# A graph layer's edge gather: three of sixteen columns moved from indirect DMAs to one-hot matmuls

## The chip, the cores and the metric

The kernel runs on one core of one Trainium2 chip. The metric is the device time of one execution in microseconds. Before the change it is 2046.08 us, the median of 3 runs (2045.63 to 2046.55).

The core has five engines that run side by side, each in the order of its own instruction stream: TensorE (PE in the profile, its weight loads PEld), VectorE (DVE), ScalarE (ACT), GpSimd (POOL) and SyncE (SP). They wait for each other by semaphores. On-chip memory is SBUF, with 128 partitions; matmuls write to PSUM[...].

## The reference

```python
# x: 6250 x 64; src, dst: 206250 edges, sorted by dst; edge_attr: 206250 x 64
h = maximum(layernorm(x), 0)
msg = relu(h[src] + edge_attr)
agg = segment_sum(msg, dst, num_segments=6250)
out = x + relu((h + agg) @ W1 + b1) @ W2 + b2
```

All is fp32. The edges are sorted by destination, so edges that lie next to each other add into nodes that lie next to each other. The source indices are random.

## The kernel before

**Groups and columns.** Edges are taken in 201 groups of 1024 (`GE`): partition p holds 8 consecutive edges (`G`), so a group is 8 columns of 128 edges. A last group of 4 columns holds the tail. The source and destination indices of all columns are loaded at the start (`src_sb`, `dst_sb`).

**Prologue.** `ln_head`, `ln_rows` and `ln_turn` compute h in chunks of 12 x 128 nodes. Each chunk is written to DRAM (`h_rows`) and is also turned by TensorE into `z`, which holds h with features on partitions and nodes along the row; the sums are added into `z`. The first 4 groups (`RAW`) gather rows of x, not of h, and are normalized after the gather (`norm_edges`), so that they need not wait for h.

**Loading.** `load(g)` issues one 256 KB load of attributes on SP's queue and, in `gather` (L133), one indirect DMA on GpSimd's queue for each column: 128 rows of 64 floats, chosen by that column's indices. The buffers `ea` and `xg` are 12 deep (`LOOK`), so gathers run ahead of the compute until no buffer is free.

**A group's compute.** `take(g+1)` lets ScalarE copy the next group's attributes into PSUM (`full`, L306). `window_sum(g)` then does the following. VectorE builds the one-hot of each edge's place in a window of 64 nodes (`oh`, L318), adds the gathered rows to `full` (L322), and ScalarE takes the relu. The message is split into three bf16 terms that add up to the fp32 value (L324 to L328, alternating between ScalarE and VectorE). TensorE sums the 8 columns by matmuls with the one-hot as the stationary operand (L333), giving a tile of 64 nodes x 3 x 64. `turn(g)` runs two groups later (`TLAG`): VectorE adds the three terms (L288) and TensorE transposes the result (L292). `sum_into_z(g)` runs six groups later (`LAG`): VectorE adds the 64 columns into `z` at a start that it reads from `dst_sb` into a register (L297); the registers are loaded for 8 groups at a time.

**Blocks.** When all edges of a block of 512 nodes have surely been summed (`READY`), `hidden` (L341, L343), `result` (L351) and `store` (L358) compute and write its output, in steps two groups apart (`blocks_behind`).

**Order.** The schedule is written by hand: each engine executes its instructions in the order in which the loop at the end of the kernel issues them. No planner moves them.

**Left-over edges.** `find_left` and `judge` look for edges that do not fit their group's window, and a slow path behind a condition handles those. With these inputs it is not entered.

Of the kernel before, what the change touches and what calls it, by code (L numbers as in the profile page):

```python
# [9 lines left out]
F32 = mybir.dt.float32  # L10
I32 = mybir.dt.int32
BF16 = mybir.dt.bfloat16
# [24 lines left out]
LOOK = 12  # L37
LAG = 6
TLAG = 2
AB = 2  # L40
TB = 4
# [7 lines left out]
def kernel(  # L49
# [18 lines left out]
    lnp = ctx.enter_context(tc.tile_pool(name="ln", bufs=2))  # L68
    edge = ctx.enter_context(tc.tile_pool(name="edge", bufs=LOOK))
    work = ctx.enter_context(tc.tile_pool(name="work", bufs=4))  # L70
# [45 lines left out]


# [18 lines left out]

    def load(g):
        ea = edge.tile([P, G, D], F32, name="ea")
        attr_load(ea, g)
        xg = edge.tile([P, G, D], F32, name="xg")  # L140
        gather(xg, src_sb[:, cols_of(g)], G if g < NG else CT, x if g < RAW else h_rows)
        return ea, xg
# [5 lines left out]

    def norm_edges(xg):
        s = lnp.tile([P, XC * R], F32, name="ln_s")  # L150
        nc.vector.tensor_reduce(s[:, :G], xg, AX.X, ALU.add)
        nc.vector.tensor_scalar_mul(s[:, :G], s[:, :G], 1.0 / D)
        nc.vector.tensor_tensor(xg, xg, s[:, :G].unsqueeze(2).to_broadcast([P, G, D]), ALU.subtract)
        sq = lnp.tile([P, XC * R, D], F32, name="ln_sq")
        nc.scalar.activation(sq[:, :G], xg, AF.Square)
        v = lnp.tile([P, XC * R], F32, name="ln_v")
        nc.vector.tensor_reduce(v[:, :G], sq[:, :G], AX.X, ALU.add)
        nc.scalar.activation(v[:, :G], v[:, :G], AF.Sqrt, bias=eps_sb, scale=1.0 / D)
        nc.vector.reciprocal(v[:, :G], v[:, :G])
        nc.vector.scalar_tensor_tensor(xg, xg, 0.0, v[:, :G].unsqueeze(2).to_broadcast([P, G, D]),  # L160
                                       op0=ALU.max, op1=ALU.mult)
# [13 lines left out]
    def ln_rows(c, xc, sq, p, n):  # L175
        v = lnp.tile([P, XC * R], F32, name="ln_v")
        nc.vector.tensor_reduce(v[:p, :n], sq[:p, :n], AX.X, ALU.add)
        nc.scalar.activation(v[:p, :n], v[:p, :n], AF.Sqrt, bias=eps_sb[:p], scale=1.0 / D)
        nc.vector.reciprocal(v[:p, :n], v[:p, :n])
        h = lnp.tile([P, XC * R, D], F32, name="ln_h", bufs=3)  # L180
        nc.vector.scalar_tensor_tensor(h[:p, :n], xc[:p, :n], 0.0,  # L181
                                       v[:p, :n].unsqueeze(2).to_broadcast([p, n, D]),
                                       op0=ALU.max, op1=ALU.mult)
        if c < NB:
            nc.sync.dma_start(
                out=h_rows[c * P * R:(c + XC) * P * R, :].rearrange("(b p r) d -> p b (r d)", p=P, r=R),
                in_=h.rearrange("p (b r) d -> p b (r d)", r=R),
            )
        else:
            nc.sync.dma_start(out=h_rows[NB * P * R:, :], in_=h[:TN, 0, :])  # L190
        return c, h

# [13 lines left out]
    for c in range(0, NB + 1, XC):  # L206
        heads.append(ln_head(c))
        if len(heads) > 1:
            rows.append(ln_rows(*heads[-2]))
        if len(rows) > 1:  # L210
            ln_turn(*rows[-2])
    rows.append(ln_rows(*heads[-1]))
    ln_turn(*rows[-2])
    ln_turn(*rows[-1])
# [26 lines left out]
    found = {}  # L241

    def find_left():
        nc.vector.tensor_scalar(left, slot, 1.0, None, op0=ALU.is_lt)
        nc.vector.scalar_tensor_tensor(left, slot, float(W), left, op0=ALU.is_gt, op1=ALU.add)
        nc.vector.scalar_tensor_tensor(left, dst_sb, 1.0, left, op0=ALU.add, op1=ALU.mult)
        nc.vector.memset(left[:TD, C + TJ:], 0.0)
        most = const.tile([P, 1], F32, name="most")
        nc.vector.tensor_reduce(most, left, AX.X, ALU.max)
        pf = psum.tile([P, R * D], F32, name="big", bufs=1)  # L250
        nc.tensor.matmul(pf[0:1, 0:1], most, ones[:, 0:1], start=True, stop=True)
        found["all"] = pf

    def judge():
        pf = found.pop("all")
# [23 lines left out]
    aggs = {}  # L279

    turned = {}
    banks = []
    turns = []

    def turn(g):
        pa = aggs.pop(g)
        rows = work.tile([W, D], F32, name="agg_rows", bufs=LAG)
        nc.vector.tensor_reduce(rows, pa.rearrange("w t d -> w d t"), AX.X, ALU.add)  # L288
        if g % TB == 0:
            turns.append(psum.tile([D, TB, W], F32, name="turned", bufs=2))  # L290
        pt = turns[-1][:, g % TB]
        nc.tensor.transpose(pt, rows, ident[:W, :W])  # L292
        turned[g] = pt

    def sum_into_z(g):
        at = window_start(g)
        nc.vector.tensor_tensor(z[:, ds(at, W)], z[:, ds(at, W)], turned.pop(g), ALU.add)  # L297

    taken = {}

    def take(g):

        n = G if g < NG else CT
# [3 lines left out]
        taken[g] = full, xg  # L307

    def window_sum(g):
        n = G if g < NG else CT  # L310
        cols = cols_of(g)
        if g + 1 <= NG:
            take(g + 1)
        full, xg = taken.pop(g)
        if g < RAW:
            norm_edges(xg)
        oh = work.tile([P, G, W], BF16, name="oh")
        nc.vector.tensor_tensor(  # L318
            oh[:, :n], slot[:, cols].unsqueeze(2).to_broadcast([P, n, W]),
            wslots.unsqueeze(1).to_broadcast([P, n, W]), ALU.is_equal)  # L320

        nc.vector.tensor_tensor(full[:, :n], full[:, :n], xg[:, :n], ALU.add)  # L322
# [5 lines left out]
        nc.vector.tensor_tensor(parts[:, :n, 2, :], full[:, :n], parts[:, :n, 1, :], ALU.subtract)  # L328
        if g % AB == 0:
            banks.append(psum.tile([W, AB, 3, D], F32, name="agg", bufs=2))  # L330
        pa = banks[-1][:, g % AB]
        for j in range(n):
            nc.tensor.matmul(pa, oh[:, j, :], parts[:, j], start=(j == 0), stop=(j == n - 1))  # L333
# [41 lines left out]

    take(0)
    for g in range(NG + 1):
        window_sum(g)
        if g >= TLAG:
            turn(g - TLAG)  # L380
        if g >= LAG:
            sum_into_z(g - LAG)
            blocks_behind(g - LAG)
        if g == 8:
            find_left()
        if g == 14:
            judge()
        if g == 15:
# [4 lines left out]
    for g in range(NG + 1 - TLAG, NG + 1):  # L393
        turn(g)
# [4 lines left out]
    for c in sorted(res):  # L399
        store(c, res.pop(c))  # L400
# [76 lines left out]
```

## Time and profile before

| | |
|---|---|
| median of 3 runs | 2046.08 us |
| profiled execution | 2045.61 us |
| its span, first to last instruction | 2043.8 us |
| instructions in it | 10215 |
| busy: TensorE, its weight loads | 402.8 us, 294.9 us |
| busy: VectorE, ScalarE, GpSimd | 669.9 us, 386.5 us, 1530.5 us |
| indirect gathers (L133) | 1580 from h_rows, 32 from x |
| moved by DMA | 112.98 MB, 55 GB/s over the span |

The profile is that of one execution. A row of its table of groups gives the line, the engine, the operation, the tiles written and read, the shapes and the count; then the busy time in us and the mean duration of one instruction in ns; then the time that the engine sat idle just before these instructions, and what ended most of that idle time. "issue" means that nothing the profile shows was waited for. Lines of the timeline give the start in us, the duration in us, the engine and the group, and in brackets the idle time before it.

### The profile page before, as it was taken

Reading aid. Unit: us, or ns where it says so; the run is one execution under the profiler, and the core shown is the slowest. Engines: PE = TensorE matmul, PEld = TensorE weight load, DVE = VectorE, ACT = ScalarE, POOL = GpSimd, SP = SyncE. Lnnn points to the kernel's source line nnn. Section 1 sums busy time; section 2 is a strip of 40 time slices with the busy share of each in tenths; the row PEclk is TensorE's granted clock in tenths of the full one; section 3 lists DMA queues with packets and bytes.
Section 4 is the critical chain, followed back from the end, with each engine's and each line's share of the span. In section 5 each row is a group of like instructions: output and inputs, shape, how many; then the busy total and the mean of one; then the engine's idle time right before and its main releaser. Section 6 shows DMA issues by size and latency. Waiting matters only on the chain. (4 is left out here: it accounts for less than half of the span.)

```text
span 2043.8 us, 10215 instructions
## 1 busy us (share of the span) xinstructions
PE 402.8 (20%) x1991; PEld 294.9 (14%) x1991; DVE 669.9 (33%) x1321; ACT 386.5 (19%) x652; POOL 1530.5 (75%) x1619
## 2 busy tenths in 40 slices
PE   2221121121121121112112112212111211211212
PEld 1111111111111111111111111111111111111111
DVE  4643333333333333332333333333333233333333
ACT  3321111111111111111111111111111111111111
POOL 7777777777777777777777777777777777777774
DMA  5221113113113113111311411311311221131121
GB/s 184 69 56 41 26 27 111 27 26 116 27 27 106 32 27 101 42 27 26 111 27 26 117 27 27 106 32 27 106 37 27 66 72 26 28 115 26 27 62 23
DMA packets 87529, 112.98 MB, mean 55 GB/s; under 512 B 30948, under 2 KB 35684, under 8 KB 87460
## 3 DMA queue, kind: packets, MB, share of 16 engines
q0 software_dynamic: 51584, 52.93, 13.3%
q1 hardware_dynamic: 34628, 57.65, 8.5%
q10 hardware_dynamic: 1248, 1.70, 0.2%
q14 instruction: 52, 0.43, 0.1%
q8 instruction: 17, 0.28, 0.1%
HBM read 108.96 MB, written 3.20 MB: 55 GB/s over the span
## 5 line engine op out<-in xcount | busy, mean ns | idle before, releaser
L133 POOL DMA_INDIRECT xg<-h_rows,src_sb x1580 | 1497.7, 948 | 481.5 <-issue 434.0
L333 PE MATMUL agg<-parts,oh 128*64 128x192 bf16 x1612 | 294.5, 363 | 1593.4 <-DVE parts L328 1593.4
L333 PEld LDWEIGHTS <-oh 128*64 128x64 bf16 x1612 | 237.7, 165 | 1634.9 <-DVE parts L328 783.6
L322 DVE TENSOR_TENSOR full<-full,xg 128x512 f32<-128x512 f32 x202 | 140.9, 698 | 957.8 <-DMA xg<-h_rows,src_sb 957.8
L324 ACT ACTIVATE parts<-full 128x512 bf16<-128x512 f32 x202 | 120.4, 596 | 1201.1 <-DVE full L322 1198.3
L325 DVE SCALAR_TENSOR_TENSOR full<-full,parts 128x512 f32<-128x512 f32 x202 | 141.1, 698 | 151.0 <-ACT parts L324 151.0
L328 DVE TENSOR_TENSOR parts<-full,parts 128x512 bf16<-128x512 f32 x202 | 139.5, 690 | 131.5 <-ACT parts L327 131.5
L306 ACT COPY full<-ea 128x512 f32<-128x512 f32 x202 | 118.6, 587 | 199.4 <-DVE parts L328 134.8
L327 ACT CAST parts<-full 128x512 bf16<-128x512 f32 x202 | 118.2, 585 | 154.6 <-DVE full L325 154.6
L318 DVE TENSOR_TENSOR oh<-slot,wslots 128x512 bf16<-128x512 f32 x202 | 135.4, 670 | 0.0
L297 DVE TENSOR_TENSOR z<-z,turned 64x64 f32 x202 | 41.2, 204 | 88.5 <-issue 86.3
L288 DVE TENSOR_REDUCE agg_rows<-agg 64x64 f32<-64x192 f32 x202 | 68.4, 339 | 0.5 <-PE agg L333 0.5
L292 PE MATMUL turned<-ident,agg_rows 64*64 64x64 f32 x202 | 63.0, 312 | 0.2 <-DVE agg_rows L288 0.2
L133 POOL DMA_INDIRECT xg<-in_x_dram,src_sb x32 | 31.7, 990 | 13.3 <-issue 9.4
L292 PEld LDWEIGHTS turned<-ident,agg_rows 64*64 64x64 f32 x202 | 25.4, 126 | 56.0 <-issue 52.4
L341 PE MATMUL big<-z,w_sb 64*64 64x512 f32 (+1 forms) x26 | 24.2, 1032 | 1.1 <-DVE z L297 0.6
L351 PE MATMUL big<-w_sb,h 64*128 64x64 f32 (+1 forms) x98 | 23.6, 418 | 1.2 <-ACT h L343 1.2
L351 PEld LDWEIGHTS big<-w_sb,h 64*128 64x128 f32 (+1 forms) x98 | 22.3, 329 | 3.2 <-ACT h L343 3.2
L199 PE MATMUL big<-ident,ln_h 128*64 128x128 f32 x48 | 12.7, 420 | 33.7 <-DVE ln_h L181 19.2
L343 ACT ACTIVATE h<-big,b_sb 64x512 f32<-64x512 f32 (+1 forms) x13 | 8.5, 656 | 56.6 <-PE big L341 56.6
L200 ACT COPY z<-big 64x512 f32<-64x512 f32 x12 | 12.6, 1051 | 11.5 <-PE big L199 11.5
L199 PEld LDWEIGHTS big<-ident,ln_h 128*64 128x64 f32 x48 | 6.4, 159 | 39.5 <-issue 19.1
(53 smaller groups left out, 69.1 us busy)
## 6 DMA issues: line engine op xcount, KB each, us to landing
ea<-in_edge_attr_dram SPq DMA_DIRECT2D x201, 256.0 KB
xg<-h_rows,src_sb POOLq DMA_INDIRECT x1580, 2.4
x_sb<-in_x_dram SPq DMA_DIRECT2D x4, 384.0 KB
h_rows<-ln_h SPq DMA_DIRECT2D x4, 384.0 KB
out_dram<-o SPq DMA_DIRECT2D x12, 128.0 KB
dst_sb<-in_dst_main_dram ACTq DMA_DIRECT2D x1, 804.0 KB
src_sb<-in_src_main_dram ACTq DMA_DIRECT2D x1, 788.0 KB
xg<-in_x_dram,src_sb POOLq DMA_INDIRECT x32, 2.5
```

The lines of the kernel that those rows point to most:

```text
L133: nc.gpsimd.indirect_dma_start(out=xg[:, j, :], out_offset=None, in_=rows[:, :], in_offset=bass.IndirectOffsetOnAxis(ap=idx[:, j:j + 1], a ...
L288: nc.vector.tensor_reduce(rows, pa.rearrange("w t d -> w d t"), AX.X, ALU.add)
L292: nc.tensor.transpose(pt, rows, ident[:W, :W])
L306: nc.scalar.copy(full[:, :n], ea[:, :n])
L318: nc.vector.tensor_tensor(oh[:, :n], slot[:, cols].unsqueeze(2).to_broadcast([P, n, W]), wslots.unsqueeze(1).to_broadcast([P, n, W]), ALU. ...
L322: nc.vector.tensor_tensor(full[:, :n], full[:, :n], xg[:, :n], ALU.add)
L324: nc.scalar.activation(parts[:, :n, 0, :], full[:, :n], AF.Relu)
L325: nc.vector.scalar_tensor_tensor(full[:, :n], full[:, :n], 0.0, parts[:, :n, 0, :], op0=ALU.max, op1=ALU.subtract)
L327: nc.scalar.copy(parts[:, :n, 1, :], full[:, :n])
L328: nc.vector.tensor_tensor(parts[:, :n, 2, :], full[:, :n], parts[:, :n, 1, :], ALU.subtract)
L333: nc.tensor.matmul(pa, oh[:, j, :], parts[:, j], start=(j == 0), stop=(j == n - 1))
L351: nc.tensor.matmul(p2[:p, k * D:(k + 1) * D], h1[:, k, :p], w2_sb, start=True, stop=True)
```

## The change

TensorE fetches some of the columns in place of GpSimd's indirect DMAs. From group 4 on, a group with an even number has its last 2 columns picked on chip and one with an odd number its last column: 3 of 16. The prologue keeps h in SBUF as three bf16 terms (`hp`, 49 sets of 128 nodes), and a table `ids` with the node number of each partition in each set. For a picked column, TensorE spreads its 128 source indices over all partitions (`spread`), VectorE compares them with `ids` in four instructions, which gives 49 one-hot matrices of 128 nodes x 128 edges, and TensorE multiplies each with its set of `hp`, adding up in one PSUM tile of 128 edges x 3 x 64 (`pick`). ScalarE puts the attributes into a fourth column of that tile, and VectorE's reduction over the four yields the sum of h and attribute for that column.

The window sum is rewritten with it: the messages stay fp32, and the message is now the stationary operand, so that the sum comes out with features on partitions. The split into bf16 terms, `turn` and its lag are gone. `sum_into_z` follows one group behind (`LAG` is 1), a block's stages follow one group apart, `judge` is part of `find_left`, `LOOK` is 10, and `one_hot(g + 1)` is built a group ahead.

```diff
-LOOK = 12
-LAG = 6
-TLAG = 2
-AB = 2
-TB = 4
+LOOK = 10
+LAG = 1
+AB = 4
+KB = NB * R + 1
+BIAS = 4096
+CUTS = (0, 13, 25, 37, KB)
...
+    node = const.tile([P, KB], I32, name="node")
+    nc.gpsimd.iota(node[:, :KB - 1].rearrange("p (b r) -> p b r", r=R), pattern=[[P * R, NB], [1, R]],
+                   base=BIAS, channel_multiplier=R)
+    nc.gpsimd.iota(node[:, KB - 1:], pattern=[[0, 1]], base=BIAS + NB * P * R, channel_multiplier=1)
+    ids = const.tile([P, KB, P], I16, name="ids")
+    hp = const.tile([P, KB, 3, D], BF16, name="hp")
+    nc.vector.memset(hp[:, KB - 1], 0.0)
...
+    def pool_cols(g):
+        if g == NG:
+            return CT
+        return G if g < RAW else G - 2 + g % 2
     def load(g):
         ea = edge.tile([P, G, D], F32, name="ea")
         attr_load(ea, g)
         xg = edge.tile([P, G, D], F32, name="xg")
-        gather(xg, src_sb[:, cols_of(g)], G if g < NG else CT, x if g < RAW else h_rows)
+        gather(xg, src_sb[:, cols_of(g)], pool_cols(g), x if g < RAW else h_rows)
         return ea, xg
...
+    def ln_parts(c, h):
+        p, k, n = (P, c * R, XC * R) if c < NB else (TN, KB - 1, 1)
+        nc.scalar.copy(hp[:p, k:k + n, 0, :], h[:p, :n])
+        rest = lnp.tile([P, XC * R, D], F32, name="ln_rest")
+        nc.vector.tensor_tensor(rest[:p, :n], h[:p, :n], hp[:p, k:k + n, 0, :], ALU.subtract)
+        nc.scalar.copy(hp[:p, k:k + n, 1, :], rest[:p, :n])
+        nc.vector.tensor_tensor(hp[:p, k:k + n, 2, :], rest[:p, :n], hp[:p, k:k + n, 1, :], ALU.subtract)
...
+        for c, h in rows:
+            ln_parts(c, h)
+    for k in range(0, KB, 7):
+        nc.scalar.copy(ids[:, k:k + 7], node[:, k:k + 7].unsqueeze(2).to_broadcast([P, 7, P]))
+    hot = ctx.enter_context(tc.tile_pool(name="hot", bufs=3))
...
-    aggs = {}
-    turned = {}
-    banks = []
-    turns = []
-    def turn(g):
-        pa = aggs.pop(g)
-        rows = work.tile([W, D], F32, name="agg_rows", bufs=LAG)
-        nc.vector.tensor_reduce(rows, pa.rearrange("w t d -> w d t"), AX.X, ALU.add)
-        if g % TB == 0:
-            turns.append(psum.tile([D, TB, W], F32, name="turned", bufs=2))
-        pt = turns[-1][:, g % TB]
-        nc.tensor.transpose(pt, rows, ident[:W, :W])
-        turned[g] = pt
+    tiles = [g * G + j for g in range(NG) for j in range(pool_cols(g), G)]
+    tile_no = {c: t for t, c in enumerate(tiles)}
+    ahead = {}
+    src16 = const.tile([P, C], I16, name="src16")
+    nc.vector.tensor_scalar_add(src16, src_sb[:, :C], float(BIAS))
+    turned = psum.tile([P, 8, P], BF16, name="turned", bufs=1)
+    def spread(t):
+        if t < len(tiles):
+            nc.tensor.transpose(turned[:, t % 8, :],
+                                src16[:, tiles[t]:tiles[t] + 1].bitcast(BF16).to_broadcast([P, P]), ident_b)
+    def pick(t):
+        oh = hot.tile([P, KB, P], BF16, name="hot")
+        at = turned[:, t % 8, :].bitcast(I16)
+        for k, to in zip(CUTS, CUTS[1:]):
+            nc.vector.tensor_tensor(oh[:, k:to], at.unsqueeze(1).to_broadcast([P, to - k, P]),
+                                    ids[:, k:to], ALU.is_equal)
+        pk = psum.tile([P, 4, D], F32, name="pick", bufs=2)
+        for k in range(KB):
+            nc.tensor.matmul(pk[:, :3], oh[:, k, :], hp[:, k], start=(k == 0), stop=(k == KB - 1))
+        return pk
...
+    aggs, hots, taken, picks, banks = {}, {}, {}, {}, []
     def sum_into_z(g):
         at = window_start(g)
-        nc.vector.tensor_tensor(z[:, ds(at, W)], z[:, ds(at, W)], turned.pop(g), ALU.add)
-    taken = {}
+        nc.vector.tensor_tensor(z[:, ds(at, W)], z[:, ds(at, W)], aggs.pop(g), ALU.add)
+    def one_hot(g):
+        n = G if g < NG else CT
+        oh = work.tile([P, G, W], F32, name="oh")
+        nc.vector.tensor_tensor(
+            oh[:, :n], slot[:, cols_of(g)].unsqueeze(2).to_broadcast([P, n, W]),
+            wslots.unsqueeze(1).to_broadcast([P, n, W]), ALU.is_equal)
+        hots[g] = oh
...
     def take(g):
-        n = G if g < NG else CT
+        n = pool_cols(g)
         ea, xg = loaded[g] if g < RAW else load(g)
         full = psum.tile([P, G, D], F32, name="full", bufs=2)
         nc.scalar.copy(full[:, :n], ea[:, :n])
-        taken[g] = full, xg
+        taken[g] = full, xg, ea
+    def pick_group(g):
+        for j in range(pool_cols(g), G if g < NG else 0):
+            t = tile_no[g * G + j]
+            spread(t + 4)
+            picks[g, j] = pick(t)
+            nc.scalar.copy(picks[g, j][:, 3], taken[g][2][:, j])
     def window_sum(g):
-        n = G if g < NG else CT
-        cols = cols_of(g)
-        if g + 1 <= NG:
-            take(g + 1)
-        full, xg = taken.pop(g)
+        n, m = (G, pool_cols(g)) if g < NG else (CT, CT)
+        full, xg, _ = taken.pop(g)
         if g < RAW:
             norm_edges(xg)
-        oh = work.tile([P, G, W], BF16, name="oh")
-        nc.vector.tensor_tensor(
-            oh[:, :n], slot[:, cols].unsqueeze(2).to_broadcast([P, n, W]),
-            wslots.unsqueeze(1).to_broadcast([P, n, W]), ALU.is_equal)
-        nc.vector.tensor_tensor(full[:, :n], full[:, :n], xg[:, :n], ALU.add)
-        parts = work.tile([P, G, 3, D], BF16, name="parts")
-        nc.scalar.activation(parts[:, :n, 0, :], full[:, :n], AF.Relu)
-        nc.vector.scalar_tensor_tensor(full[:, :n], full[:, :n], 0.0, parts[:, :n, 0, :],
-                                       op0=ALU.max, op1=ALU.subtract)
-        nc.scalar.copy(parts[:, :n, 1, :], full[:, :n])
-        nc.vector.tensor_tensor(parts[:, :n, 2, :], full[:, :n], parts[:, :n, 1, :], ALU.subtract)
+        nc.vector.tensor_tensor(full[:, :m], full[:, :m], xg[:, :m], ALU.add)
+        for j in range(m, n):
+            nc.vector.tensor_reduce(full[:, j], picks.pop((g, j)).rearrange("p t d -> p d t"), AX.X, ALU.add)
+        msg = work.tile([P, G, D], F32, name="msg")
+        nc.scalar.activation(msg[:, :n], full[:, :n], AF.Relu)
+        oh = hots.pop(g)
         if g % AB == 0:
-            banks.append(psum.tile([W, AB, 3, D], F32, name="agg", bufs=2))
+            banks.append(psum.tile([D, AB, W], F32, name="agg", bufs=1))
         pa = banks[-1][:, g % AB]
         for j in range(n):
-            nc.tensor.matmul(pa, oh[:, j, :], parts[:, j], start=(j == 0), stop=(j == n - 1))
+            nc.tensor.matmul(pa, msg[:, j, :], oh[:, j, :], start=(j == 0), stop=(j == n - 1))
         aggs[g] = pa
...
-    hid, res = {}, {}
+    hid = {}
     def blocks_behind(g):
-        for c in sorted(res):
-            if READY[c] + 4 <= g:
-                store(c, res.pop(c))
         for c in sorted(hid):
-            if READY[c] + 2 <= g and not res:
-                res[c] = result(c, hid.pop(c))
+            store(c, result(c, hid.pop(c)))
         for c in range(NB):
             if READY[c] == g:
                 hid[c] = hidden(c)
+    for t in range(4):
+        spread(t)
     take(0)
+    one_hot(0)
     for g in range(NG + 1):
-        window_sum(g)
-        if g >= TLAG:
-            turn(g - TLAG)
         if g >= LAG:
             sum_into_z(g - LAG)
             blocks_behind(g - LAG)
+        window_sum(g)
+        if g + 1 <= NG:
+            take(g + 1)
+            pick_group(g + 1)
+            one_hot(g + 1)
         if g == 8:
             find_left()
-        if g == 14:
-            judge()
-        if g == 15:
+        if g == 9:
             for c in range(NB):
                 nc.vector.tensor_tensor(x_sb[:, c], x_sb[:, c],
                                         b2_sb.unsqueeze(1).to_broadcast([P, R, D]), ALU.add)
             nc.vector.tensor_tensor(x_sb[:TN, NB, 0, :], x_sb[:TN, NB, 0, :], b2_sb[:TN], ALU.add)
-    for g in range(NG + 1 - TLAG, NG + 1):
-        turn(g)
     for g in range(NG + 1 - LAG, NG + 1):
         sum_into_z(g)
         blocks_behind(g)
```

More of the change, by code (lines that the diff above doesn't have):

```diff
@@ L11 @@
 I32 = mybir.dt.int32
+I16 = mybir.dt.int16
 BF16 = mybir.dt.bfloat16
@@ L67 @@
     const = ctx.enter_context(tc.tile_pool(name="const", bufs=1))
-    lnp = ctx.enter_context(tc.tile_pool(name="ln", bufs=2))
     edge = ctx.enter_context(tc.tile_pool(name="edge", bufs=LOOK))
-    work = ctx.enter_context(tc.tile_pool(name="work", bufs=4))
+    work = ctx.enter_context(tc.tile_pool(name="work", bufs=3))
     dram = ctx.enter_context(tc.tile_pool(name="dram", bufs=1, space=bass.MemoryType.DRAM))
@@ L115 @@
     nc.vector.tensor_copy(wslots, slots[:, :W])
+    ident_b = const.tile([P, P], BF16, name="ident_b")
+    nc.vector.tensor_copy(ident_b, ident)
+    node = const.tile([P, KB], I32, name="node")
[5 more added lines that the diff above has]
+    nc.vector.memset(hp[:, KB - 1], 0.0)
     h_rows = dram.tile([N, D], F32, name="h_rows")
@@ L147 @@
     loaded = [load(g) for g in range(RAW)]
[L149 to L161, printed above, removed]
     def ln_head(c):
@@ L179, in ln_rows @@
         nc.vector.reciprocal(v[:p, :n], v[:p, :n])
-        h = lnp.tile([P, XC * R, D], F32, name="ln_h", bufs=3)
+        h = lnp.tile([P, XC * R, D], F32, name="ln_h", bufs=5)
         nc.vector.scalar_tensor_tensor(h[:p, :n], xc[:p, :n], 0.0,
@@ L205 @@
     heads, rows = [], []
[L206 to L214, printed above, removed]
+    with tc.tile_pool(name="ln", bufs=2) as lnp:
+        for c in range(0, NB + 1, XC):
+            heads.append(ln_head(c))
+            if len(heads) > 1:
+                rows.append(ln_rows(*heads[-2]))
+            if len(rows) > 1:
+                ln_turn(*rows[-2])
+        rows.append(ln_rows(*heads[-1]))
+        ln_turn(*rows[-2])
+        ln_turn(*rows[-1])
+        for c, h in rows:
[3 more added lines that the diff above has]
+    hot = ctx.enter_context(tc.tile_pool(name="hot", bufs=3))
     base = const.tile([1, NG + 1], F32, name="base")
@@ L240 @@
     flag = const.tile([1, 1], I32, name="flag")
-    found = {}
     def find_left():
@@ L251, in find_left @@
         nc.tensor.matmul(pf[0:1, 0:1], most, ones[:, 0:1], start=True, stop=True)
-        found["all"] = pf
-    def judge():
-        pf = found.pop("all")
         done = const.tile([1, NG + 1], F32, name="done")
@@ new lines, in norm_edges @@
+    def norm_edges(xg):
+        s = hot.tile([P, G], F32, name="raw_s")
+        nc.vector.tensor_reduce(s, xg, AX.X, ALU.add)
+        nc.vector.tensor_scalar_mul(s, s, 1.0 / D)
+        nc.vector.tensor_tensor(xg, xg, s.unsqueeze(2).to_broadcast([P, G, D]), ALU.subtract)
+        sq = work.tile([P, G, D], F32, name="msg")
+        nc.scalar.activation(sq, xg, AF.Square)
+        v = hot.tile([P, G], F32, name="raw_v")
+        nc.vector.tensor_reduce(v, sq, AX.X, ALU.add)
+        nc.scalar.activation(v, v, AF.Sqrt, bias=eps_sb, scale=1.0 / D)
+        nc.vector.reciprocal(v, v)
+        nc.vector.scalar_tensor_tensor(xg, xg, 0.0, v.unsqueeze(2).to_broadcast([P, G, D]),
+                                       op0=ALU.max, op1=ALU.mult)
@@ L398 @@
     hid[NB] = hidden(NB)
-    for c in sorted(res):
-        store(c, res.pop(c))
     for c in sorted(hid):
```

## The prediction

> **What bounds the kernel now.** I read the page of groups first, then one steady stretch as a timeline, then the chain of waits. GpSimd issues one indirect gather per column of 128 edges and does nothing else:
>
> ```profile
> PE 402.8 (20%) x1991; PEld 294.9 (14%) x1991; DVE 669.9 (33%) x1321; ACT 386.5 (19%) x652; POOL 1530.5 (75%) x1619
> ...
> L133 POOL DMA_INDIRECT xg<-h_rows,src_sb x1580 | 1497.7, 948 | 481.5 <-issue 434.0
> ...
> L322 DVE TENSOR_TENSOR full<-full,xg 128x512 f32<-128x512 f32 x202 | 140.9, 698 | 957.8 <-DMA xg<-h_rows,src_sb 957.8
> ```
>
> 75% busy looks like slack, but the timeline (start, duration, engine, group, idle before it) shows that the other quarter is a fixed 0.30 us of issue after every gather:
>
> ```profile
> 1000.27 0.95 POOL L133 DMA_INDIRECT xg<-h_rows,src_sb  x1 [0.30 <-issue]
> 1001.52 0.94 POOL L133 DMA_INDIRECT xg<-h_rows,src_sb  x1 [0.30 <-issue]
> 1002.77 0.95 POOL L133 DMA_INDIRECT xg<-h_rows,src_sb  x1 [0.30 <-issue]
> ...
> 1007.66 1.49 PE L333 MATMUL agg<-parts,oh 128*64 128x192 bf16 x8 [8.05 <-DVE parts L328]
> ```
>
> One gather per 1.25 us, so 1612 gathers take 2015 us; they start at 5.7 us, a few cost 1.5 us, and the last ends at 2026.0. The chain at the end of the run then needs only the last gather's landing (2.4 us) and about 15 us of other work. VectorE waits 957.8 us for gathers: it is behind POOL, not beside it. A group of eight columns costs 8 x 1.25 = 10.0 us.
>
> **POOL's part of the change.** Groups 4 to 200 gather 6 (even) or 7 (odd) columns instead of 8: 99 x 2 + 98 x 1 = 296 gathers go to TensorE and 1316 stay. 296 x 1.25 = 370 us leave POOL. If POOL still set the end: 2043.8 - 370 = 1674 us. What replaces them must fit under 16.25 us per pair of groups to earn all of it, and under 20.0 to earn anything.
>
> **What one picked column costs.** (a) VectorE compares: 4 instructions of 1664, 1536, 1536, 1536 elements, all 16-bit, one operand in PSUM. No row shows such a compare. The row with one element per 1.04 ns (512 elements 0.698 us, 256 in 0.432, so 0.165 us fixed) gives 6.9 us with 0.07 us of overlap between neighbours; two elements per tick give 0.96 + 3 x 0.895 = 3.64 us. [...] I take 3.64 and keep 6.9 as a rival. (b) TensorE: 49 pairs of a 128-column weight load and a 192-column bf16 matmul: 296 x 49 = 14504 pairs. The nearest row is L333: eight matmuls of the same 192 columns in 1.49 us, each 0.363 long, so (1.49 - 0.363) / 7 = 0.161 us apart. [...] The granted-clock column reads 1.00 throughout[...]. TensorE will now be busy some 80% with gaps below 2 us, so I take full clock: half of 0.161 is 0.080[...]. No run here shows it yet. [...] I take 0.087: the row shows hiding, but of a load half as wide under twice the time. (c) ScalarE copies the attribute column into PSUM, some 0.21 us (from 587 ns for 512 and 376 ns for 256 elements); VectorE reduces 192 to 64, 0.339 us by L288. (d) TensorE turns the index column, about 0.12 us.
>
> **What the window sum costs.** The three-part split goes: on VectorE L325, L328 (0.698 + 0.690) and L288, on ScalarE L327 (0.585). That was 2.3 us of VectorE per group, all under POOL's 10 us, worth nothing in time; its use is room: compares 7.3 us in an even group, plus one-hot 0.60, window add 0.27, add 0.57 and reduces 0.6 make 9.3, where the split would have pushed it past 11. The sum becomes 8 fp32 matmuls, each two records (as the 98 records of L351 for 49 matmuls). L341 shows such records 0.886 us apart for 512 columns[...]: 16 x 0.078 = 1.25 us [...].
>
> **The order that now counts.** TensorE runs in program order: sum of group g, then the picks of g+1, then the sum of g+1. That sum needs the relu, which needs the reduces, which need the last pick. So between picks and sum TensorE idles once per group: drain of the last matmul 0.20 (0.363 - 0.161), copy 0.21, reduce 0.34, relu 0.60 (L324), handoffs 0.23 (gaps of 0.04 to 0.11 in the timeline): 1.58 us. Before, the lags of 2 and 6 groups kept such latencies off every path; now the lag is 1. Per group, with p for the pair:
> - even: 1.58 + 1.25 + 2 x 0.12 + 98p = 3.07 + 98p, at 0.087: 11.6 us
> - odd: 1.58 + 1.25 + 0.12 + 49p = 2.95 + 49p: 7.2 us
>
> VectorE's 9.3 and 5.4 lie under these. 18.8 us per pair is above POOL's 16.25: TensorE's chain becomes the bound and POOL waits for free buffers (10 deep, which therefore cost nothing).
>
> **The ends and the exceptions.** Prologue: ScalarE finishes turning h at 48.0; then come, on ScalarE and VectorE alternately, the bf16 parts of h: (0.81 + 0.98 + 0.81 + 0.15) x 4 = 11 us and 1 for the tail (L170's 0.98 for 768 elements, ScalarE's 0.83 ns per element), then 7 id copies of 0.91 = 6.4. The first group is normalized from about 66 instead of 51.7, four raw groups cost about 8.8 each because the window add now waits for its own group's sum: picks start at 101. The load of window starts stalls VectorE 3.5 us, 25 times (86.3 us of issue at L297). It falls in odd groups: 3.64 + 0.60 + 3.5 + 0.27 + 0.63 = 8.6 before the reduce, where TensorE would be ready at 6.8: 25 x 1.8 = 45. A block's hidden and result stages, formerly 2 and 4 groups behind, now put a ScalarE relu (0.68) ahead of the group's, and a store (0.41) and its matmuls ahead of the add: about 3 us x 12 = 36. The left-over search and the bias adds: 8. Tail after the last group: 23 (15 now, plus the last sum).
>
> Sum: 101 + 99 x 3.07 + 98 x 2.95 + 45 + 36 + 8 + 23 = 806, plus 14504p. With p = 0.087: 806 + 1262 = 2068 us against the span of 2043.8; the medians lie 2.3 above the span, so 2070, 1.2% slower. It meets the old span at p = 0.0853.
>
> **Rivals.**
> - *Pairs at the array's pace (faster).* Loads hide fully, p = 0.083 [...]: 806 + 1204 - 69 = 1941. [...] It decides from p below 0.0853, or at 0.087 from a sum below 1.12 us.
> - *Loads not hidden (slower).* [...]
> - *Compares at one element per tick.* VectorE becomes the bound: even 13.9 + 0.60 + 0.27 + 0.57 + 0.6 = 15.9, odd 8.8: 99 x 15.9 + 98 x 8.8 = 2436, plus 101 + 88 + 36 + 8 + 23 = 2692.
> - *The clock stays at half.* p = 0.161, sum 2.5: 806 + 246 + 2335 = 3390. [...]
> - *POOL stays the bound.* 1674 plus the longer prologue, some 1700. It would need a pair of groups in 16.25, so p below 0.070, under what 192 columns take at twice the row's clock. I give it 0.03.
>
> **Chances.** TensorE's chain with p from 0.082 to 0.095 and the sum near 1.25: 0.52, own range 1995 to 2180, of which 0.19 lies below the old time, 0.04 within 0.2% and 0.29 above. Full hiding 0.13; loads not hidden 0.20; compares at 1x 0.08; half clock or a similar pace of issue 0.04; POOL 0.03. Faster 0.35, same 0.04, slower 0.61. (0.2% is about what three runs from 2045.63 to 2046.55 can tell.) The range 1910 to 2500 leaves out the last three and the lower tail, near 0.18.
>
> **What would show it.** Compares about 0.9 us long (1.8: the 1x rival). L315 matmuls 0.087 apart in long bursts. TensorE idle some 1.6 us per group, ended by the relu. POOL's gathers no longer 1.25 apart but held up by xg's release. VectorE waiting for the ScalarE attribute copy ahead of the reduces. The prediction fails if p leaves 0.083 to 0.092, or if a group's sum takes 2 us: each 0.01 us of p is 145 us of time, each 0.1 us of the chain per group 20.

## The result, and the profile after

The changed kernel takes 2401.9 us, the median of 4 runs (2401.08 to 2404.1), against 2045.88 for the kernel before beside it: a ratio of 1.1741 (1.1721 to 1.1762), 17% slower. The forecast was slower, 2070 us: a loss of 24 us was forecast, and 356 came. The time lies in the forecast's range, 332 us above its value.

The page of the changed kernel, first by busy time and clock, then the chain by line, then its costliest groups:

```profile
PE 1676.9 (70%) x18201; PEld 1540.2 (64%) x18201; DVE 1510.9 (63%) x2208; ACT 309.8 (13%) x763; POOL 1251.4 (52%) x1325
...
PEclk9988999989999999999999999999998999999999
...
PE pick L315 55%; DVE hot L311 13%; PE agg L377 10%; ACT msg L371 5%; DVE full L369 4%; PE turned L304 2%; ACT pick L360 2%; POOL xg L146 1%; DVE full L367 1%; PE big L395 1%; PE big L385 1%; DVEq L287 1%; PE big L212 0%; ACT z L213 0%; DMA x_sb<-in_x_dram 0%
...
L146 POOL DMA_INDIRECT xg<-h_rows,src_sb x1284 | 1217.7, 948 | 1029.7 <-DVE full L367 678.3
L315 PE MATMUL pick<-hp,hot 128*128 128x192 bf16 x14504 | 1355.1, 258 | 327.1 <-DVE hot L311 327.1
...
L311 DVE TENSOR_TENSOR hot<-turned,ids 128x1536 bf16<-128x1536 int16 (+1 forms) x1184 | 1070.8, 967 | 677.1 <-PE turned L304 675.0
L377 PE MATMUL agg<-oh,msg 128*64 128x64 f32 x3224 | 243.7, 232 | 334.2 <-ACT msg L371 334.2
...
L304 PE MATMUL turned<-ident_b,src 128*128 128x128 bf16 x296 | 67.4, 230 | 3.1 <-DVE src L298 3.1
```

Three things are to be seen. GpSimd is no longer the bound: its gathers now stand idle 678.3 us for VectorE's release of a buffer, where before they had a steady pace. TensorE is busy only 70%, and its idle time has two halves of nearly the same size: 334.2 us ahead of the sum (L377, ended by the relu), which the prediction had, and 327.1 us ahead of the picks (L315, ended by the compares), which it did not have. And the compares (L311) wait 675.0 us for TensorE's small index transpose (L304). So TensorE waits for VectorE, and VectorE for TensorE. The mean granted clock is 0.939. The 1.00 of the kernel before can't be set beside it: its trace has no change of the clock on record, yet its matmuls of 192 columns stand 0.161 us apart, where the changed kernel's are 0.083 apart at full clock and 0.160 at half.

A group with one pick in the timeline of the changed kernel (start, duration, engine, group, idle time before it):

```profile
1012.61 1.15 PE L377 MATMUL agg<-oh,msg 128*64 128x64 f32 x16 [1.46 <-ACT msg L371]
...
1013.69 0.23 PE L304 MATMUL turned<-ident_b,src 128*128 128x128 bf16 x1
1013.96 3.62 DVE L311 TENSOR_TENSOR hot<-turned,ids 128x1664 bf16<-128x1664 int16 x4 [2.03 <-PE turned L304]
...
1015.04 4.22 PE L315 MATMUL pick<-hp,hot 128*128 128x192 bf16 x49 [1.12 <-DVE hot L311]
...
1019.35 0.22 ACT L360 COPY pick<-ea 128x64 f32<-128x64 f32 x1 [6.35 <-PE pick L315]
...
1019.60 0.43 DVE L369 TENSOR_REDUCE full<-pick 128x64 f32<-128x256 f32 x1 [0.33 <-ACT pick L360]
1020.06 0.60 ACT L371 ACTIVATE msg<-full 128x512 f32<-128x512 f32 x1 [0.50 <-DVE full L369]
...
1020.71 1.15 PE L377 MATMUL agg<-oh,msg 128*64 128x64 f32 x16 [1.46 <-ACT msg L371]
```

The whole group is one chain on TensorE: sum (1.08 us to the next start), transpose (0.23), 1.12 us of nothing on TensorE while VectorE makes the first quarter of the one-hots, pick (4.22), 1.46 us of nothing until the relu: 1.08 + 0.23 + 1.12 + 4.22 + 1.46 = 8.11, and the two sums start 8.10 us apart. VectorE was idle 2.03 us before these compares, though the transposed index of *this* pick had lain in PSUM for four picks. But `pick_group` issues `spread(t + 4)` and then `pick(t)`, and both slots lie in the one tile `turned`. The compares of pick t start when the transpose for pick t + 4 ends (1013.69 + 0.23 = 1013.92; compares at 1013.96), and that transpose stands on TensorE behind the sum. In a group with two picks the second one's transpose stands behind the first pick, with the same 1.12 us.

### The profile page after: what moved, and what is told of

Same layout as the page of the kernel before. It is cut to its first block, busy times and chain, and to the rows that moved or that the text cites. A ratio compares the mean times of both kernels' runs of the same rounds, so it can differ in the third digit from the quotient of the medians.

```text
span 2400.2 us, 43505 instructions
## 1 busy us (share of the span) xinstructions
PE 1676.9 (70%) x18201; PEld 1540.2 (64%) x18201; DVE 1510.9 (63%) x2208; ACT 309.8 (13%) x763; POOL 1251.4 (52%) x1325
## 4 chain that ended last, share of the span: by engine, by line
PE 68%; DVE 18%; ACT 7%; issue 3%; POOL 1%; DVEq 1%; DMA 1%; ACTq 0%; SPq 0%
PE pick L315 55%; DVE hot L311 13%; PE agg L377 10%; ACT msg L371 5%; DVE full L369 4%; PE turned L304 2%; ACT pick L360 2%; POOL xg L146 1%; DVE full L367 1%; PE big L395 1%; PE big L385 1%; DVEq L287 1%; PE big L212 0%; ACT z L213 0%; DMA x_sb<-in_x_dram 0%
## 5 line engine op out<-in xcount | busy, mean ns | idle before, releaser
L146 POOL DMA_INDIRECT xg<-h_rows,src_sb x1284 | 1217.7, 948 | 1029.7 <-DVE full L367 678.3
L315 PE MATMUL pick<-hp,hot 128*128 128x192 bf16 x14504 | 1355.1, 258 | 327.1 <-DVE hot L311 327.1
L315 PEld LDWEIGHTS <-hot 128*128 128x128 bf16 x14504 | 1276.4, 103 | 385.8 <-DVE hot L311 373.0
L311 DVE TENSOR_TENSOR hot<-turned,ids 128x1536 bf16<-128x1536 int16 (+1 forms) x1184 | 1070.8, 967 | 677.1 <-PE turned L304 675.0
L377 PE MATMUL agg<-oh,msg 128*64 128x64 f32 x3224 | 243.7, 232 | 334.2 <-ACT msg L371 334.2
L377 PEld LDWEIGHTS agg<-oh,msg 128*64 128x64 f32 x3224 | 215.0, 144 | 386.7 <-ACT msg L371 386.7
L369 DVE TENSOR_REDUCE full<-pick 128x64 f32<-128x256 f32 x296 | 128.1, 433 | 118.3 <-ACT pick L360 105.4
L371 ACT ACTIVATE msg<-full 128x512 f32<-128x512 f32 x202 | 120.1, 595 | 142.6 <-DVE full L369 132.7
L341 DVE TENSOR_TENSOR oh<-slot,wslots 128x512 f32<-128x512 f32 x202 | 136.6, 676 | 0.0
L367 DVE TENSOR_TENSOR full<-full,xg 128x384 f32<-128x384 f32 (+1 forms) x202 | 118.8, 588 | 5.7 <-issue 4.8
L304 PE MATMUL turned<-ident_b,src 128*128 128x128 bf16 x296 | 67.4, 230 | 3.1 <-DVE src L298 3.1
L304 PEld LDWEIGHTS <-src 128*128 128x128 bf16 x296 | 28.6, 97 | 17.5 <-DVE src L298 3.6
```

What stands on the lines that cost most here:

```text
L146: nc.gpsimd.indirect_dma_start(out=xg[:, j, :], out_offset=None, in_=rows[:, :], in_offset=bass.IndirectOffsetOnAxis(ap=idx[:, j:j + 1], a ...
L304: nc.tensor.transpose(turned[:, t % 8, :], src16[:, tiles[t]:tiles[t] + 1].bitcast(BF16).to_broadcast([P, P]), ident_b)
L311: nc.vector.tensor_tensor(oh[:, k:to], at.unsqueeze(1).to_broadcast([P, to - k, P]), ids[:, k:to], ALU.is_equal)
L315: nc.tensor.matmul(pk[:, :3], oh[:, k, :], hp[:, k], start=(k == 0), stop=(k == KB - 1))
L341: nc.vector.tensor_tensor(oh[:, :n], slot[:, cols_of(g)].unsqueeze(2).to_broadcast([P, n, W]), wslots.unsqueeze(1).to_broadcast([P, n, W]) ...
L367: nc.vector.tensor_tensor(full[:, :m], full[:, :m], xg[:, :m], ALU.add)
```

## The experiments

The first theory, A in the expectations: the wait of the compares for the newest index transpose makes the loss. It keeps VectorE's compares from running beside TensorE's sum and picks, so TensorE idles before each pick. Its rivals are that TensorE's own work is too much (pairs, clock, the copy, reduce and relu ahead of the sum), that the rewritten sum with a lag of one group costs the time, and that 3 of 16 is simply too large a share.

Two sets of runs, the first eight below, fell on chips where the kernel before takes 2433 us, not 2046. In their traces the instructions of VectorE and GpSimd last as long as on the first chip (compares 967 ns and gathers 947 ns in the changed kernel), but engines stand still for stretches that the profile puts down to nothing on this core, so the numbers of those sets are compared only among themselves.

**Transposes left out.** The eight slots are filled once, ahead of the loop, and every later transpose is left out; picks after the eighth use stale indices, so that this measures time only.

```diff
-            spread(t + 4)
...
-    for t in range(4):
+    for t in range(8):
         spread(t)
```

> Leaves out the transposes of index columns after the eighth: every later pick compares with one of the first eight columns, so its sums are not the reference's; all other work stays. Theory A: in the changed kernel the compares of a pick wait for the index transpose of four picks later, which shares their PSUM tile and stands on TensorE behind the group's sum or the pick before; so TensorE idles 1.12 us before each pick (327 us) and spends 67 us on the transposes. Without them: compares start at once, TensorE's idle before L315 nearly gone, time 2000 to 2080. Theory B: the time is TensorE's own pace (half clock in a part of the picks, the copy-reduce-relu chain), and the wait only shows slack of VectorE: 2300 to 2340, the transposes' own time less.

Measured: 2744.75 us against 2432.68, ratio 1.127 (1.1211 to 1.1326).

**One pick per group** (2 of 16 columns):

```diff
-        return G if g < RAW else G - 2 + g % 2
+        return G if g < RAW else G - 1
```

> One picked column per group instead of 1.5 on average; nothing else changes. Theory A: every group costs TensorE the 8.1 us that a one-pick group takes in the changed kernel, below POOL's 7 x 1.25 = 8.75, so POOL is the bound again: 2044 - 197 x 1.25 = 1798 plus 10 to 20 for the longer prologue, 1800 to 1830. Theory B (a pick costs more than the gather it replaces, at any share): at best 2046, above it if TensorE's clock falls further with more gaps.

Measured: 2671.79 us, 1.0964 (1.0873 to 1.1054), with a granted clock of 0.77.

**Index through SBUF.** ScalarE copies each transposed index into a ring in SBUF, and the compares read that copy, so they no longer read `turned`.

```diff
...
+            idx[t] = hot.tile([P, P], I16, name="idx", bufs=3)
+            nc.scalar.copy(idx[t], turned[:, t % 8, :].bitcast(I16))
...
-        at = turned[:, t % 8, :].bitcast(I16)
+        at = idx.pop(t)
...
-            spread(t + 4)
+            spread(t + 2)
...
-    for t in range(4):
+    for t in range(2):
```

> The changed kernel with its whole computation, but ScalarE copies each transposed index column to SBUF and the compares read it there; the transposes go two picks ahead. Theory A: the compares no longer wait for TensorE, time 2040 to 2110 (the first experiment's plus the transposes). Theory B: 2380 to 2420. If two SBUF operands slow GpSimd's gathers, their spacing rises above 1.25 us while compares run, at no cost to the time as POOL is not the bound.

Measured: 2578.87 us, 1.06 (1.0554 to 1.0646). Its page:

```profile
L146 POOL DMA_INDIRECT xg<-h_rows,src_sb x1284 | 1416.2, 1103 | 999.0 <-DVE full L369 627.6
L317 PE MATMUL pick<-hp,hot 128*128 128x192 bf16 x14504 | 1390.9, 261 | 24.3 <-issue 22.5
```

TensorE's wait before the picks is gone (24.3 us), with every pick and every transpose still there. What it brings along: a gather takes GpSimd 1103 ns in the mean, not 948.

**No picks**, all columns gathered, the rest of the change kept:

```diff
-        return G if g < RAW else G - 2 + g % 2
+        return G
```

> No column is picked: the rewritten fp32 sum, the lag of one group and the longer prologue alone, with all 1612 gathers on GpSimd. Theory A: all of that lies under POOL's 10 us per group: 2046 to 2075, what is above 2046 being POOL waiting for buffers in the prologue. Rival: the lag of one and the fp32 sum cost time themselves: above 2100.

Measured: 2405.99 us, 0.9878 (0.9829 to 0.9927).

For a scale on these chips, the changed kernel itself ran in the next set, with nothing edited:

> The changed kernel once more, as the yardstick for the runs beside it. On the first chip it took 1.174 of the time before. If the chip is like the first: 2400. If instructions are held up here as on the chip of the first four experiments, where the kernel before took 2433 and engines stood still with nothing to wait for, the ratio is what counts.

Measured: 3331.93 us against 2434.81, 1.3673 (1.3541 to 1.3805). The same program stands 17% behind on one chip and 37% behind on another. Against this 1.3673, the index ring's 1.06 and the left-out transposes' 1.127 both speak for A, though they come from another chip. Two kernels of the first set were repeated beside it.

> As the first experiment, beside the changed kernel on the same chip. The transposes of index columns after the eighth are left out, so that picked columns compare with stale indices and their sums are not the reference's. Theory A (the compares queue behind the transpose that shares their PSUM tile): TensorE's idle time before the picks falls from 327 us to under 30 and the transposes' 67 us go; some 350 us less than the changed kernel, 2000 to 2080 where that takes 2400. Theory B (TensorE's own pace): no more than 70 to 100 us less.

Measured: 2740.94 us, the faster of two runs (the other took 2789.46), 1.126 without an interval.

> One picked column per group. Theory A: a one-pick group costs TensorE 8.1 us, below POOL's 8.75, so POOL is the bound: 1800 to 1830, faster than before by about 11%. Theory B (a pick costs more than the gather it replaces): 2046 or more.

Measured: 2711.22 us, 1.1125 (1.1045 to 1.1204).

**Picks ahead.** The whole computation in another order: the picks of group g + 1 stand on TensorE ahead of the sum of group g, and the transposes directly behind the picks. The attribute copies come after the relu, three pick buffers are used, and the window's slot numbers move to SBUF, which makes room in PSUM for the third.

```diff
...
-        pk = psum.tile([P, 4, D], F32, name="pick", bufs=2)
+        pk = psum.tile([P, 4, D], F32, name="pick", bufs=3)
...
+        for t in picked(g):
+            picks[g, tiles[t] % G] = pick(t)
+        for t in picked(g + 1):
+            spread(t)
...
+        if g + 1 <= NG:
+            pick_group(g + 1)
         if g >= LAG:
             sum_into_z(g - LAG)
...
             take(g + 1)
-            pick_group(g + 1)
+            pick_attrs(g + 1)
```

> The whole computation with 3 of 16 columns picked, reordered: the picks of group g+1 stand ahead of the sum of group g on every engine, the index transposes follow directly behind the picks, ScalarE's attribute copies go behind the relu; three pick buffers, and the window numbers move from PSUM to SBUF to make room. Theory A (queues, not TensorE's pace, cost the time): per pair of groups TensorE has 147 x 0.083 + 2 x 1.15 + 0.7 = 15.2 and VectorE about 15.3, POOL 16.25: POOL is the bound again and the time is 1674 plus 15 to 60 for the prologue, 1690 to 1740. Theory B (its pace): TensorE's half clock alone adds 100 us and the chain stays: 2100 to 2300.

Measured: 2553.18 us, 1.0513 (1.042 to 1.0605).

The direction was plain, but the standstills on these chips (in the run with transposes left out, 462 spacings above 0.3 us inside picks, 396 us together) hid the sizes. All further runs fell on a chip where the kernel before takes 2046.6 us and no such spacing occurs inside a pick.

**Transposes left out, on the chip of 2046.6 us:**

> Third placing of this kernel, hoping for a chip on which the kernel before takes 2046 as at first: index transposes after the eighth left out, picked columns compare with stale indices, sums not the reference's. Theory A there: 2000 to 2080, TensorE's idle time before the picks under 30 us. Theory B: 2300 to 2340.

Measured: 1902.02 us (1898.01 to 1906.04), 0.9298 (0.9273 to 0.9323). Its page:

```profile
L315 PE MATMUL pick<-hp,hot 128*128 128x192 bf16 x14504 | 1245.6, 248 | 0.0
```

The same 14504 pairs, no idle time before them: 500 us less than the changed kernel, and more than was expected. The row says why: the pairs' own busy time fell as well, from 1355.1 to 1245.6 us. The granted clock rose to 0.984. That TensorE has too much work by itself is thereby refuted; that the transposes' own 67.4 us are the cost cannot account for 500 either.

**One pick per group, there:**

> One picked column per group. Theory A, where the kernel before takes 2046: 1800 to 1830. Where it takes 2430: 2680 as twice before, since TensorE's instructions are held up.

Measured: 1944.45 us, 0.951 (0.9494 to 0.9526), faster than before but over 100 us above the expectation. Its page:

```profile
PEclk9997888888889889888888888888888888988888
...
L315 PE MATMUL pick<-hp,hot 128*128 128x192 bf16 x9653 | 1036.5, 279 | 216.1 <-DVE hot L311 216.1
```

A third fewer pairs, and each takes longer (279 ns). The clock granted is 0.876. With less work in each group but the same two gaps (1.12 and 1.40 us), TensorE falls to half clock more often: the mean pick takes 5.015 us from its first start to its last, against 3.97 at full clock, 197 x 1.045 = 206 us. The expectation had the clock full.

**Picks ahead, there:**

> Picks ahead of the sum, 3 of 16 columns. Theory A, where the kernel before takes 2046: 1690 to 1740. Where it takes 2430: 2550 as before.

Measured: 1712.59 us (1712.23 to 1714.32), 0.8375 (0.8361 to 0.8389), as expected; it beats both kernels. Its page (busy time, chain by engine, the sum's row), then its timeline:

```profile
PE 1530.0 (89%) x18203; PEld 1457.9 (85%) x18203; DVE 1486.8 (87%) x2208; ACT 293.6 (17%) x763; POOL 1287.4 (75%) x1325
...
PE 34%; POOL 22%; DVE 16%; issue 14%; DMA 11%; ACT 3%; DVEq 1%; SPq 0%; POOLq 0%; ACTq 0%
...
L382 PE MATMUL agg<-oh,msg 128*64 128x64 f32 x3224 | 236.8, 228 | 110.8 <-ACT msg L376 110.8
```

```profile
1005.29 7.14 DVE L311 TENSOR_TENSOR hot<-turned,ids 128x1664 bf16<-128x1664 int16 x8
...
1005.47 1.15 PE L382 MATMUL agg<-oh,msg 128*64 128x64 f32 x16 [0.56 <-ACT msg L376]
...
1006.55 8.26 PE L315 MATMUL pick<-hp,hot 128*128 128x192 bf16 x98
```

The compares of the next picks (1005.29) start ahead of the sum and run beside it, so the 98 pairs follow the sum without a gap. Instructions on TensorE and VectorE are those of the changed kernel, up to two transposes; only their order and buffers differ. The chain is now shared between three engines: TensorE's load is near GpSimd's.

**Picks ahead with one pick per group** (the edit above, and `G - 1`):

> Picks ahead of the sum, one column per group (2 of 16): a third fewer matmuls than with 3 of 16. Where the kernel before takes 2046: POOL's 8.75 per group is the bound, 1800 to 1830, no better than the same share in the old order. Where it takes 2430, because instructions are held up: if the number of TensorE's instructions sets the loss, less than with 3 of 16 (2550), some 2300 to 2450; if it is the chain between engines, above 2550.

Measured: 1840.89 us, 0.9001 (0.8986 to 0.9016), a little above the expectation. The chain by engine on its page:

```profile
POOL 54%; DMA 22%; issue 19%; DVE 2%; PE 2%; ACT 1%; DVEq 0%; POOLq 0%; SPq 0%; ACTq 0%
```

Here GpSimd is the bound again: 1415 gathers x 1.25 = 1769 us, and its gathers from h_rows are 981 ns long in the mean, not 948 (33 ns x 1383 = 46). So 3 of 16 isn't too large a share: with the wait gone, the larger share is the faster one.

**Only the place of the transposes.** The changed kernel with one edit: the transposes for the next group's picks stand directly behind this group's picks, not between the sum and the picks.

```diff
...
-        for j in range(pool_cols(g), G if g < NG else 0):
-            t = tile_no[g * G + j]
-            spread(t + 4)
+        for t in picked(g):
+            j = tiles[t] % G
             picks[g, j] = pick(t)
             nc.scalar.copy(picks[g, j][:, 3], taken[g][2][:, j])
+        for t in picked(g + 1):
+            spread(t)
...
```

> The changed kernel with one thing moved and nothing left out: the index transposes for the next group's picks stand directly behind this group's picks on TensorE, ahead of its sum, instead of one ahead of each pick. Where the kernel before takes 2046. Theory A (the place of the transpose alone sends the compares behind the sum): compares start with the last reduce, TensorE has no idle time before picks, transposes lie in its idle stretch before the sum: 1890 to 1930. Theory C (what the ablation won was the transposes' own time and work left out): 2250 to 2350.

Measured: 1908.58 us (1906.34 to 1910.33), 0.933 (0.9315 to 0.9346), as expected. Its page, then its timeline:

```profile
L315 PE MATMUL pick<-hp,hot 128*128 128x192 bf16 x14504 | 1244.5, 248 | 0.0
...
L311 DVE TENSOR_TENSOR hot<-turned,ids 128x1536 bf16<-128x1536 int16 (+1 forms) x1184 | 1059.8, 965 | 0.0
L381 PE MATMUL agg<-oh,msg 128*64 128x64 f32 x3224 | 239.1, 230 | 315.5 <-ACT msg L375 315.5
```

```profile
1016.27 7.13 DVE L311 TENSOR_TENSOR hot<-turned,ids 128x1664 bf16<-128x1664 int16 x8
...
1017.04 1.15 PE L381 MATMUL agg<-oh,msg 128*64 128x64 f32 x16 [1.34 <-ACT msg L375]
...
1018.12 8.26 PE L315 MATMUL pick<-hp,hot 128*128 128x192 bf16 x98
```

The compares start at 1016.27, ahead of the relu and the sum, and wait for nothing. (The transposes now run one or two picks ahead, not four, which can only leave less room.) Idle time before the picks went from 327.1 us to 0, and that before the sum stayed (334.2 and 315.5). The place of one 0.2 us instruction turns 17% slower into 7% faster. What still separates this kernel from the picks-ahead order is the idle time before the sum, 315.5 us here and 110.8 there: that is about the 196 us between the two.

**Fillers.** The changed kernel with its waits, and 12 more matmuls at the start of each pick, into the same tile from a constant operand. Their result is overwritten, as the first real pair starts the tile anew.

```diff
         pk = psum.tile([P, 4, D], F32, name="pick", bufs=2)
+        for _ in range(12):
+            nc.tensor.matmul(pk[:, :3], ident_b, hp[:, 0], start=True, stop=True)
         for k in range(KB):
```

> The changed kernel, its waits as they are, with 12 more matmuls ahead of each pick, on data that are ready, into the pick's own tile, whose first real matmul overwrites them. They fill about 1.0 us of the 1.12 us in which TensorE waits for the first compare. Theory D (the gaps let TensorE's clock fall to half, which lengthens picks from 3.97 to 4.33 us on average): the granted clock rises from 0.94 to above 0.98, picks come back to 4.0, some 80 to 100 us less: 2300 to 2330, with 3552 matmuls more. Rival (the half clock does not come from these gaps): 2400 to 2430.

Measured: 2305.81 us (2304.95 to 2306.1), 1.1269 (1.125 to 1.1288), as expected. Its timeline:

```profile
1013.90 1.15 PE L315 MATMUL pick<-hp,ident_b 128*128 128x192 bf16 x12
1014.10 3.62 DVE L311 TENSOR_TENSOR hot<-turned,ids 128x1664 bf16<-128x1664 int16 x4 [2.03 <-PE turned L304]
...
1015.18 4.22 PE L317 MATMUL pick<-hp,hot 128*128 128x192 bf16 x49
```

The fillers occupy the time in which TensorE would wait; the compares still wait 2.03 us for the transpose, and the pick starts no earlier. Yet 3552 matmuls more make the kernel 96 us faster than the changed one, and the granted clock goes from 0.939 to 0.988. That is the size of the half clock by itself, with the wait left in place.

**No picks, there:**

> No column picked: the rewritten sum, the lag of one and the longer prologue alone, on a chip where the kernel before takes 2046: 2046 to 2075 if they lie under POOL's 10 us per group; above 2100 if the lag of one costs time itself.

Measured: 2039.35 us, 0.9966 (0.9951 to 0.9981), just below the expectation. The fp32 sum, the lag of one group and the longer prologue cost nothing while GpSimd sets the pace. They are not where the 500 us come from; once TensorE sets the pace, the lag of one group costs the 334 us before the sum, which the prediction had.

## Why the prediction was wrong

**The step that failed** is the sentence that VectorE's 9.3 and 5.4 us "lie under these", under TensorE's 11.6 and 7.2. By length they fit. By order they can't: between a sum and the next pick the compares hold TensorE up. The prediction did count the transpose under (d), as about 0.12 us of TensorE's time; it asked what it costs and not who is queued behind it and who waits for it. The loss that this wait brings, by its parts, from the changed kernel and the one with the transposes left out (1902 us):

- TensorE idle before picks, 292 x 1.12 = 327 us.
- The transposes themselves, 67 us.
- Half clock: the mean pick is 4.333 us against 4.017, 296 x 0.316 = 94 us. The fillers give 96.

Together 488 of 2401.9 - 1902.0 = 500 us. The remaining 12 are not assigned. Against the prediction's own sum, the wait adds 327 us and half clock 296 x (4.333 - 3.97) = 107; the pairs (58) and the register loads (45) came out lower than taken. That makes 331 of the 332 us missed, so near in part by chance, as the smaller differences below are left out.

That the kernel is slower, as forecast, is luck. With the pair at the measured 0.083 us, the prediction's own sum gives 806 + 1204 = 2010 us, faster than before; what made it slower are the two terms that it did not have.

**The clock** is the second wrong term: "busy some 80% with gaps below 2 us, so I take full clock". TensorE was busy 70%, since the wait was missed. The trace records 64 stretches at half clock, 296 us together; 50 last 3.41 us, and all but one of the others a multiple of it. Between 200 and 1700 us the picks show 43 stretches of pairs at half pace, the median of them 21 spacings, 3.3 us long. No trace had shown that gaps below 2 us leave the clock full. Of the gaps that lie wholly in that part of the run the longest is 2.7 us, and the mean of those above 0.3 us is 1.28; the half clock came all the same, at a cost of 94 us.

The trace also shows what the half clock went with. Cut it into steps of 3.41 us, the length of most of those stretches, and take TensorE's busy share in each. At full clock, each of the 56 steps below 50% was followed by half clock, 8 of the 151 between 50 and 64%, and none of the 379 above. At half clock, full clock came back after each of the 63 steps above 77% and after none of the 22 below. So in this trace no single gap decides, but how much of such a step is idle. Two gaps of 1.46 and 1.12 us, 1.31 us apart, can leave 1.31 of 3.41 us busy, 38%; one gap of 1.46 leaves 57%. With the other gap filled, the granted clock was 0.988.

**The pair p** was right at its lower end: within picks at full clock the spacing is 83.0 ns (median), near half of the 161 in the row of L333, which is 80.5. The 87 taken was the author's estimate, 4 ns x 14504 = 58 us too much. So the failure named in advance (p outside 0.083 to 0.092) did not happen, nor did the other (a sum of 2 us). The list of what could go wrong left out the one wait that did.

**The compares** took the shorter of the two times considered, as taken: on the page split by shape the changed kernel has

```profile
L311 DVE TENSOR_TENSOR hot<-turned,ids 128x1536 bf16<-128x1536 int16 x888 | 792.3, 948 | 0.0
L311 DVE TENSOR_TENSOR hot<-turned,ids 128x1664 bf16<-128x1664 int16 x296 | 303.2, 1024 | 677.1 <-PE turned L304 675.0 <-issue 2.0
```

128 elements more cost 76 ns, 0.59 ns each: near the 0.52 of two elements per tick of the 1.04 ns that the prediction read from fp32 rows, with an operand in PSUM. Four of them take 3.62 us (taken: 3.64). The rival's 6.9 us did not appear. The second row also shows the wait sitting wholly on the first instruction of each four.

**The idle time before the sum** was predicted at 1.58 us per group, 0.20 of it the drain of the last matmul, which the profile counts as busy. Against the other 1.38 the timeline shows 1.46. Within it the reduction takes 0.43 us, not 0.34: it reads four columns of 64, and the estimate was made for three. The sum itself was estimated at 1.25 us and takes 1.15, with the next instruction starting 1.08 after it.

**Order and bound** were right: TensorE's chain sets the end (68% of the chain is its own, 18% VectorE's), GpSimd waits for buffers, picks start at 100.2 us (predicted 101). The 45 us for register loads did not come: the addition to `z` shows 8.7 us of issue, where it had 86.3. The loads now run beside the compares. One of 1.84 us starts at 922.95, the compares at 922.92 for 3.62 us, and TensorE's idle time before the next sum is 1.58 us there, not 1.46.

**The group, as predicted and measured.** Odd: predicted at p = 0.083 2.95 + 49 x 0.083 = 7.02, measured 8.10; the wait is 1.12, the transpose 0.11 above, the sum 0.17 below. Even, the group from 997.47 to 1012.61 in the trace: 15.14, of which 1.65 is one pick at half clock (5.87 against 4.22); the other 13.49 stand against 3.07 + 98 x 0.083 = 11.20, with two waits of 1.12.

**The rival of 1941 us**, with p = 0.083, was given 0.13. With the wait gone, the kernel stands at 1908.6: its p is the measured 83.0 ns, and the change would have been faster in this order. That the number is so near is in part luck: it took 69 us off for shorter sums, an estimate of which 0.17 x 197 = 33 came (1.08 us to the next start, against 1.25), and its 45 us of register loads did not come. The rival in which GpSimd stays the bound, some 1700 us, needed a shorter TensorE chain; the picks-ahead order gives it by taking the latencies out, not by a smaller p, and ends at 1712.6.

**What stays open.** Why the compares of pick t wait for the transpose of pick t + 4 and not only for their own is not shown. The eight slots are one tile in PSUM; slots in tiles of their own were not tried. That this wait is the cause is shown, by removing it in three ways (transposes left out, moved behind the picks, index copied to SBUF, the last only on a chip of 2433 us). The standstills on the two chips of 2433 us are not explained by any run here.

## What to carry to other kernels

An operation that is cheap by itself can still be the place where two engines take turns: here index transposes of 0.23 us each, queued behind the sum or a pick, kept the compares waiting 675.0 us. For each small instruction that feeds another engine, look up what stands ahead of it in its own queue, and who waits for it; lengths that fit under one another say nothing until the order allows it. That the slots were filled four picks ahead did not help here, as the compares started only when the newest transpose into the tile of all eight had ended (1013.92 and 1013.96); with the refill directly behind the last long work it delayed nobody, and the idle time before the picks went from 327.1 us to 0. And price gaps on TensorE twice, once as time and once as clock: here the gap before the picks cost 327 us and the half clock 94, and it was the busy share over some 3.4 us that went with the clock, not the longest gap.

## What the runs showed of the hardware that was not expected

- Gaps of 1.1 to 1.5 us, twice in 8 us, cost TensorE's full clock: 0.939 with 3 picks per two groups, 0.876 with 2 (less work between the same gaps), 0.988 with the gap before the pick filled by useless matmuls, which made the kernel 96 us faster. In the changed kernel the clock followed TensorE's busy share in steps of 3.41 us: below 50% it was lost each time, above 64% never. That is one trace, and no limit for other kernels.
- With both operands of the compares in SBUF, GpSimd's gathers took 1103 ns in the mean, with one operand in PSUM 948 (155 ns x 1284 = 199 us of GpSimd's time). The 1103 are from a chip of 2433 us, where the kernel with transposes left out kept 946. The trace agrees in detail: the 431 gathers that run beside these compares for over 0.3 us take 1396 ns in the mean, those beside no VectorE instruction 943. The picks-ahead order, on the chip of 2046.6 us, has a mean of 976. It puts the second operand of the window one-hot build in SBUF, and its longer gathers are those beside that build: 1073 ns in the mean, against 950 in the kernel with only the transposes moved, where that operand lies in PSUM; those beside the compares take 944 in both.
- The same program was 17% behind on one chip and 37% on another, with VectorE's and GpSimd's instructions of the same length and a granted clock of 0.81 where it had 0.939. A ratio found on one chip doesn't carry to a chip where engines stand still between instructions.
